# Attention and a GRU on one core: another order for the last batch, two more batches turned early, roots of norms ahead of GpSimd's normalisation

## The chip, the core and the metric

The kernel runs on one core of a Trainium2 chip. A core has TensorE (PE, matrix products; its weight loads are listed as PEld), VectorE (DVE), ScalarE (ACT), GpSimd (POOL) and SyncE (SP), each with an instruction queue that it works through in order. Products land in PSUM, eight banks of 2 KB per partition; all else lives in SBUF. The metric is the device time of one execution in microseconds.

## The reference

All arrays are float32. There are 16 batches of 256 positions of 512 features, and one row of conditions for each batch. The first half is attention with 16 heads of 32 features, the second a GRU over the 256 positions:

```python
scale, shift = split(cond @ W_emb + b_emb)
xn  = rms_norm(x, g_norm) * (1 + scale) + shift
q, k, v = heads(xn @ W_qkv)
q, k = rms_norm(q, g_q), rms_norm(k, g_k)          # per head
attn = softmax(q @ k.T * 32 ** -0.5)
o = attn @ v
x = x + o + o @ W_out
...
gi = x_t @ W_ih + b_ih ; gh = h @ W_hh + b_hh       # 256 steps
r = sigmoid(gi_r + gh_r) ; z = sigmoid(gi_z + gh_z)
n = tanh(gi_n + r * gh_n) ; h = (1 - z) * n + z * h
out_t = x_t + h
```

## The kernel before

**Attention, by batch and group.** A batch has two tiles of 128 positions. A group is four heads, so that a batch has four groups (g = 0 to 3) of 128 features. `logits` (L269) makes a group's four tiles of 128 x 512 logits, one in each of the PSUM banks lg0 to lg3. `maxima` (L292) takes the row maxima on VectorE, `exps` (L296) the exponentials and their sums on ScalarE: eight instructions of 256 columns. `normalize` (L306) takes the reciprocal of the sums on VectorE and has GpSimd multiply the eight halves by it, in place. In the next group's time `turn` (L316) transposes the normalised weights on TensorE, 64 rows at a time, into four banks; `put_turned` (L331) copies those to `attnT` in SBUF (one buffer), "v" on VectorE and "a" on ScalarE; `weigh` (L340) multiplies by v, and `put_weighed` (L356) copies the result into `oT`, which gathers [feature, position, batch] of all batches.

**The projections of the next batch ride along.** `slot0` to `slot3` (L375, L415, L436, L465) are the four groups of batch b, with the work of batch m = b + 1 written in between by hand: projections to q, k and v (`project`, L208: one step is four products of 128 x 32 by 512 columns, recorded as eight), the squares and sums of q and k, their roots and normalisation (`norm_qk`), and their turn into qT and kT (`turn_qk`, `put_qk`). Batch b + 2's x is turned (`turn_x`, `put_x`) in slot 0, and batch b + 3's is normalised in slots 1 to 3 (`norm_first`, `norm_apply`; the latter also loads the x of two batches later on SP's queue). For batch 0 and for batch 2's x there is nothing earlier: batch 0's slot 0 does all of batch 2's normalisation and turn.

**Roots.** `Rsqrt.first` (L138) makes the mean on VectorE (m) and, on ScalarE, exp(-0.5 ln) (L142, L143). `Rsqrt.second` (L145) refines it with three VectorE operations on small tiles (L147, L148, L150). In slots 1 and 2 `normalize` stands ahead of `second`.

**The banks.** Beside lg0 to lg3 there are four single banks A, X, Y, Z. q and k of the second tile, for instance, stand in Z and Y until `norm_qk` has read them, and the turn of q and k takes "ZY" next.

**The last batch** (b = 15) has no batch to project. `slot_last` (L492) turns the group before, takes maxima and exponentials, copies the turned weights (three on VectorE, one on ScalarE), normalises and weighs; in the last group half of the normalisation is VectorE's. Behind the loop the last group is turned and weighed.

**The GRU.** The output projection of 16 positions (`output_step`, wo, which has the identity added for the residual) and the input projection (`input_step`, wih) of a group of positions come as filler in the recurrence of the group before; for the first group they stand alone ahead of it: L670, first "o", then "gi". `put_block` (L680) transposes 8 positions of x into xT; `put_output` (L701) adds the output projection to it. The gates' products (L732) take three PSUM banks, "o" and "gi" two each, out of pools that are opened when attention's pools are closed.

**Order.** Inside `tc.manual_schedule` (L508, L779) TensorE, VectorE, ScalarE and GpSimd keep the order in which the program is written. SP, which issues most of the DMAs, is ordered by the scheduler. In the first part, weights and x are loaded in the order: four pieces of conditions (ScalarE's queue), w_emb (L75, both queues), x of batch 0, b_emb and g_norm (`rows`, L96, L97, SP's queue), then w_qkv (L103) by thirds, with x of batch 1 between the second and third. `rows` are transposed (L524) ahead of the embedding product (L528).

Of the kernel before, what the change touches and what calls it, by code (L numbers as in the profile page):

```python
# [19 lines left out]
def kernel(  # L20
# [51 lines left out]

    we = wpool.tile([P, KC, 2 * D], F32, tag="w_a", name="we")
    for k in range(KC):
        (nc.sync, nc.scalar)[k % 2].dma_start(we[:, k, :], w_emb[k * P : (k + 1) * P, :])  # L75

    work = ctx.enter_context(ExitStack())
    p1 = work.enter_context(tc.tile_pool(name="p1", bufs=1))
    p2 = work.enter_context(tc.tile_pool(name="p2", bufs=2))
    small = work.enter_context(tc.tile_pool(name="small", bufs=4))  # L80
    ps_lg = work.enter_context(tc.tile_pool(name="ps_lg", bufs=1, space=PSUM))
    ps = work.enter_context(tc.tile_pool(name="ps", bufs=1, space=PSUM))

# [8 lines left out]

    rows = p1.tile([12, P], F32, tag="qkn", name="rows", bufs=4)
    nc.sync.dma_start(rows[0:8, :], b_emb.rearrange("(m c) -> m c", c=P))  # L96
    nc.sync.dma_start(rows[8:12, :], g_norm.rearrange("(m c) -> m c", c=P))  # L97
    rows_b = p1.tile([26, P], F32, tag="qkn", name="rows_b", bufs=4)
# [170 lines left out]
    def logits(b, g):  # L269

        w = Group()
        w.b, w.g = b, g
        w.lg = [
            ps_lg.tile([P, NT, T], F32, tag=f"lg{i}", name=f"lg_{b}_{g}_{i}") for i in range(HG)
        ]
        for n in range(NT):
            for i in range(HG):
                r = slice(i * DH, (i + 1) * DH)
                nc.tensor.matmul(  # L279
                    w.lg[i][:, n, :],  # L280
                    qT[r, g, n * P : (n + 1) * P],
                    kT[r, g, :],
                    start=True,
                    stop=True,
                )
        w.neg = small.tile([P, HG, NT], F32, tag="neg", name=f"neg_{b}_{g}")
        w.den = small.tile([P, HG, NT], F32, tag="den", name=f"den_{b}_{g}")
        w.rden = small.tile([P, HG, NT], F32, tag="rden", name=f"rden_{b}_{g}")
        w.attn = [None] * HG
        return w  # L290
# [15 lines left out]
    def normalize(w, heads=range(HG), engine=nc.gpsimd):  # L306
        r = slice(heads[0], heads[-1] + 1)
        nc.vector.reciprocal(w.rden[:, r, :], w.den[:, r, :])  # L308
        for i in heads:
            for n in range(NT):  # L310
# [3 lines left out]
                )  # L314

    def turn(w, banks=("lg0", "lg1", "lg2", "lg3")):  # L316


        if w is None:
            return  # L320
        w.tp = [tile_ps(f"tpa_{w.b}_{w.g}_{i}", banks[i], (P, R, NT, NT, QR)) for i in range(HG)]
        for i in range(HG):
            for n in range(NT):
                for k in range(NT):
                    turn_block(
                        [w.tp[i // R * R + r][:, i % R, k, n, :] for r in range(R)],
                        w.attn[i][:, n, k * P : (k + 1) * P],
                    )
        w.attnT = p1.tile([P, HG, NT, T], F32, tag="attnT", name=f"attnT_{w.b}_{w.g}")

    def put_turned(w, engines):  # L331

        if w is None:
            return
        for i, e in enumerate(engines):
            h, r = i // R * R, i % R
            dst = w.attnT[:, h : h + R].rearrange("p h k (n r c) -> p h k n r c", n=NT, r=R)[:, :, :, :, r]
            (nc.scalar.copy if e == "a" else nc.vector.tensor_copy)(dst, w.tp[i])  # L338

# [15 lines left out]

    def put_weighed(w):  # L356
        if w is None:
            return
        nc.scalar.copy(oT[:, w.g, :, w.b], w.o)  # L359

# [14 lines left out]
    def slot0(b, w, prev, st):  # L375
        m = b + 1
        if b == 0:
# [3 lines left out]
            exps(w, range(HG))  # L381
            put_x(m, 0, st.tpx)
            put_v(b, 1, st.v1)
            st.q = project(m, 0, 0, range(KC), "A")
            norm_first(2)
            batches[2].rs.first()
            normalize(w)
            norm_apply(2, batches[2].rs.second())
            st.k = project(m, 0, 1, (0, 1), "X")
            tpx = turn_x(2, "YZ")  # L390
            put_x(2, 1, tpx)
            st.s0 = Stats(m, 0)
            st.s0.add(0, st.s0.square(0, st.q))
            put_x(2, 0, tpx)
            return
# [19 lines left out]
    def slot1(b, w, prev, st):  # L415
# [12 lines left out]
        st.s0.rs.first()  # L428
        normalize(w)
        st.s1 = Stats(m, 1)  # L430
        st.sq = st.s1.square(0, st.q1)
        weigh(prev, "Y")
        put_weighed(prev)
        st.rstd = st.s0.rs.second()

    def slot2(b, w, prev, st):  # L436
# [15 lines left out]
        if b + 3 < B:  # L452
            batches[b + 3].rs.first()
        normalize(w)
        weigh(prev, "X")
# [6 lines left out]
        st.accs = (st.q1, k)  # L462
        st.rstd = st.s1.rs.second()

    def slot3(b, w, prev, st):  # L465
# [25 lines left out]

    def slot_last(g, w, prev):  # L492

        turn(prev, "AXYZ")
        maxima(w, range(HG))
        exps(w, range(HG))
        put_turned(prev, "vvva")
        if g < NG - 1:
            normalize(w)
        else:  # L500
            normalize(w, (0, 1))
            normalize(w, (2, 3), nc.vector)
        weigh(prev, "A")
        put_weighed(prev)

    E = mybir.EngineType
    ORDERED = {E.PE, E.DVE, E.Activation, E.Pool}
    with tc.manual_schedule(engines=ORDERED):  # L508
# [12 lines left out]
        nc.vector.tensor_copy(h0T, tp)  # L521
        cols = const.tile([P, 38], F32, name="cols")
        tp = tile_ps("tp_rows", "Y")
        nc.tensor.transpose(tp[:, :12], rows, ident[:12, :12])  # L524
        nc.vector.tensor_copy(cols[:, :12], tp[:, :12])
        for k in range(KC):
            for j in range(4):
# [5 lines left out]
                    stop=(k == KC - 1),  # L533
                )
        norm_first(0)
        batches[0].rs.first()
        norm_apply(0, batches[0].rs.second())
        emb = p1.tile([P, 8, 32], F32, tag="sq", name="emb")
        nc.vector.transpose(emb.rearrange("p m b -> p (m b)"), pe)
# [16 lines left out]
        for c in range(KC):  # L556
            put_x(0, 0, tpx, (c,))
            put_x(0, 1, tpx, (c,), nc.scalar)
        q = project(0, 0, 0, range(KC), "Y")
        k = project(0, 0, 1, range(KC), "Z")  # L560
        tp = tile_ps("tp_rows_b", "lg3")
        nc.tensor.transpose(tp[:, :26], rows_b, ident[:26, :26])
# [6 lines left out]
        s0 = Stats(0, 0)  # L569
        s0.add(0, s0.square(0, q))  # L570
        s0.add(1, s0.square(1, k))
        s0.rs.first()
        norm_first(1)
        qk = norm_qk(0, 0, (q, k), s0.rs.second())
        batches[1].rs.first()
        q = project(0, 1, 0, range(KC), "A")
        s1 = Stats(0, 1)
        s1.add(0, s1.square(0, q))
        norm_apply(1, batches[1].rs.second())
        k = project(0, 1, 1, range(KC), "X")  # L580
        tq = turn_qk(0, 0, qk, ("lg0", "lg1"))
        tpx = turn_x(1, ("Z", "lg3"))
        v = project(0, 0, 2, range(KC), "Y")
        s1.add(1, s1.square(1, k))
        s1.rs.first()
        put_qk(0, 0, tq, nc.vector)
        put_qk(0, 1, tq, nc.scalar)
        put_x(1, 1, tpx, engine=nc.scalar)
        qk = norm_qk(0, 1, (q, k), s1.rs.second())
# [3 lines left out]
        put_qk(1, 1, tq, nc.scalar)  # L593
        put_v(0, 0, v)
        st.tpx = tpx

        prev = None
        for b in range(B):
            for g in range(NG):
                w = logits(b, g)  # L600
                if b + 1 < B:
                    (slot0, slot1, slot2, slot3)[g](b, w, prev, st)
                else:
                    slot_last(g, w, prev)
                prev = w
        turn(prev)
        put_turned(prev, "vava")
        weigh(prev, "X")
        put_weighed(prev)

# [29 lines left out]
    gru = ctx.enter_context(tc.tile_pool(name="gru", bufs=2))  # L640
    ps_g = ctx.enter_context(tc.tile_pool(name="ps_g", bufs=1, space=PSUM))
    ps_i = ctx.enter_context(tc.tile_pool(name="ps_i", bufs=2, space=PSUM))
    ps_o = ctx.enter_context(tc.tile_pool(name="ps_o", bufs=2, space=PSUM))

# [8 lines left out]
    gates = []  # L653
    for name in ("r", "z", "n"):
        gt = ps_g.tile([P, P], F32, tag=f"g{name}", name=f"g{name}")
        nc.vector.memset(gt, 0.0)
        gates.append(gt)

    TI = 16
    NI = T // TI  # L660
# [30 lines left out]
    def output_step(grp, i):  # L691

        m, k = divmod(i, KC)
        if k == 0:
            acc["o"] = ps_o.tile([P, TI * B], F32, tag="o", name=f"o_{grp}_{m}")
        product(
# [8 lines left out]
    def input_step(grp, i):  # L705
# [4 lines left out]
        if k == 0:  # L710
            acc["i"] = ps_i.tile([P, TI * B], F32, tag="gi", name=f"gi_{grp}_{m}")
        product(acc["i"], wih, m, k, xTs[grp][:, k].rearrange("p t b -> p (t b)"))
# [45 lines left out]
    def store_last(y, tl, n):  # L758

        tp = ps_o.tile([P, KC, P], F32, tag="o", name=f"tpy_{tl}")  # L760
        for q in range(KC):
# [17 lines left out]
    with tc.manual_schedule(engines=ORDERED):  # L779
        for i in range(TI // TG):  # L780
            put_block(i)
        for i in range(KC * KC):
            output_step(0, i)
            if i % KC == KC - 1:
                put_output(0, i // KC)
        for i in range(TI // TG, 2 * TI // TG):
# [97 lines left out]
```

## Time and profile before

| What | us |
| --- | --- |
| median of 3 runs (lowest, highest) | 1790.54 (1789.55, 1792.69) |
| the profiled execution, whole | 1791.88 |
| its span | 1790.1 |
| first logits of batch 0 start at | 36.52 |
| batch 0, slots 0 and 1 last | 11.18 and 11.70 |
| logits of batch 15 start at | 593.93 |
| first output projection starts at | 633.33 |
| first input projection starts at | 640.25 |
| recurrence starts at | 661.19 |

Busy over the span: TensorE 1731.6 us (97%), VectorE 1144.7 (64%), ScalarE 817.2 (46%), GpSimd 315.2 (18%). Shares of the whole span say little here, since the span has parts with different limits: a first part of loads and batch 0's projections, fifteen batches with projections in between, a last one without, and the recurrence, which takes 63% of the time. So the profile is read by stage. A chain of waits gives, in order of time, what each step waited for last; its columns are start, length, engine, tile, line and number of instructions. A table of stages gives each engine's busy time, the clock that TensorE was granted (1.00 is full) and the DMA engines' share. TensorE's products are pipelined, so a busy TensorE may still be stretched by a lower clock.

### The profile page before, as it was taken

To read this page: it belongs to the slowest core of one execution; us is meant where nothing else is said; L and a number is where in the kernel's file an instruction comes from. 1 tells how busy PE (TensorE), PEld (TensorE's weight loads), DVE (VectorE), ACT (ScalarE), POOL (GpSimd) and SP (SyncE) were. 2 spreads that over 40 slices of the span, in tenths; PEclk is the share of its full clock that TensorE was granted. 3 is DMA by queue.
4 is the path that set the end of the run, shared out by engine and by line. 5 is a ranking of instruction groups with operands and counts; after the bars stand their busy time and mean duration, and the time that the engine had idled before them with its cause. 6 is when DMAs were issued, how large, how long until landed. Compare 5 with 4: busy or idle time off the path is not lost.

```text
span 1790.1 us, 91923 instructions
## 1 busy us (share of the span) xinstructions
PE 1731.6 (97%) x40755; PEld 1190.4 (66%) x40755; DVE 1144.7 (64%) x3703; ACT 817.2 (46%) x2760; POOL 315.2 (18%) x769
## 2 busy tenths in 40 slices
PE   7999999999999799999999999999999999999975
PEld 2444444444444468888888888888888888888864
DVE  4777777777777635656656656566566666566555
ACT  4677777777777623333333332333333333333322
POOL 0343444433344400000000000000000000000000
PEclk9999999999999899999999999999999999999999
DMA  7200000000000110110011011001100100000000
GB/s 266 54 14 14 14 26 14 14 14 14 13 2 2 72 26 10 22 22 16 16 23 20 16 20 23 16 16 22 22 16 17 23 13 10 15 10 10 10 15 14
DMA packets 146222, 43.73 MB, mean 24 GB/s; under 512 B 137899, under 2 KB 138031, under 8 KB 145823
## 3 DMA queue, kind: packets, MB, share of 16 engines
q1 hardware_dynamic: 145375, 36.74, 8.8%
q8 instruction: 320, 5.24, 1.2%
q10 hardware_dynamic: 448, 1.10, 0.2%
q14 instruction: 79, 0.65, 0.1%
HBM read 29.41 MB, written 8.39 MB: 21 GB/s over the span
## 4 chain that ended last, share of the span: by engine, by line
PE 88%; DVE 8%; ACT 2%; issue 1%; DMA 0%; DVEq 0%; ACTq 0%; SPq 0%
PE gi L670 18%; PE qkv L214 15%; PE gr L732 13%; PE gn L732 13%; PE gz L732 12%; PE o L670 6%; PE tpa L188 3%; PE lg L279 3%; PE o L348 3%; DVE neg L294 2%; PE tpqk L188 1%; ACT attn L300 1%; DVE attnT L338 1%; DVE qkn L240 1%; DVE tr L744 1%
## 5 line engine op out<-in xcount | busy, mean ns | idle before, releaser
L670 PE MATMUL gi<-xT,wih 128*32 128x256 f32 x6144 | 364.6, 379 | 0.0
L214 PE MATMUL qkv<-wq,xnT 128*32 128x512 f32 x3072 | 355.9, 597 | 0.9 <-DVE xnT L206 0.7
L311 POOL TENSOR_SCALAR attn<-attn,rden 128x256 f32<-128x256 f32 x508 | 232.6, 480 | 394.6 <-DVE rden L308 267.7
L732 PE MATMUL gr<-whh,h 128*16 128x128 f32 x8160 | 272.2, 274 | 23.7 <-DVE h L836 23.5
L732 PEld LDWEIGHTS gr<-whh,h 128*16 128x16 f32 x8160 | 200.5, 96 | 105.8 <-DVE h L836 105.8
L838 POOL TENSOR_TENSOR y<-xT,h 128x64 f32<-128x64 f32 x255 | 81.9, 321 | 1069.2 <-DVE h L836 1031.9
L300 ACT ACTIVATE attn<-lg,neg 128x256 f32<-128x256 f32 x512 | 234.8, 485 | 77.1 <-DVE neg L294 61.3
L732 PE MATMUL gn<-whh,h 128*16 128x128 f32 x8160 | 269.5, 273 | 0.0
L732 PE MATMUL gz<-whh,h 128*16 128x128 f32 x8160 | 269.5, 273 | 0.0
L670 PEld LDWEIGHTS gi<-xT,wih 128*32 128x32 f32 x6144 | 195.9, 110 | 100.9
L807 ACT ACTIVATE r<-r 128x64 f32<-128x64 f32 x256 | 65.8, 257 | 377.7 <-DVE r L806 377.7
L744 DVE STREAM_TRANSPOSE tr<-gr 128x128 f32<-128x128 f32 x256 | 81.1, 317 | 237.6 <-PE gr L732 237.6
L732 PEld LDWEIGHTS gn<-whh,h 128*16 128x16 f32 x8160 | 224.7, 97 | 0.0
L732 PEld LDWEIGHTS gz<-whh,h 128*16 128x16 f32 x8160 | 224.7, 97 | 0.0
L214 PEld LDWEIGHTS qkv<-wq,xnT 128*32 128x32 f32 x3072 | 87.3, 109 | 181.8 <-issue 156.4
L294 DVE TENSOR_REDUCE neg<-lg 128x2 f32<-128x512 f32 x256 | 158.6, 680 | 52.4 <-PE lg L279 52.4
L714 ACT ACTIVATE gi<-gi,cols 128x256 f32<-128x256 f32 x192 | 91.2, 475 | 166.8 <-PE gi L670 166.8
L744 DVE STREAM_TRANSPOSE tr<-gn 128x128 f32<-128x128 f32 x256 | 81.1, 317 | 76.0 <-PE gn L732 76.0
L670 PE MATMUL o<-oT,wo 128*32 128x256 f32 x2048 | 121.7, 379 | 0.7 <-ACT oT L359 0.7
L338 DVE COPY attnT<-tpa 128x512 f32<-128x512 f32 x132 | 84.7, 684 | 54.0 <-ACT sq L225 37.2
L300 ACT ACTIVATION_READ_ACCUMULATOR attn<-lg,neg 128x1 f32 x512 | 110.8, 216 | 0.0
L813 ACT ACTIVATE n<-n 128x64 f32<-128x64 f32 x256 | 65.6, 256 | 98.8 <-DVE n L812 96.1
(102 smaller groups left out, 1743.4 us busy)
## 6 DMA issues: line engine op xcount, KB each, us to landing
x<-in_x_dram SPq DMA_DIRECT2D x16, 512.0 KB, 3.7
xin<-in_x_dram SPq DMA_DIRECT2D x256, 32.0 KB, 1.9
out_dram<-osb SPq DMA_DIRECT2D x248, 32.0 KB, 1.9
wq<-in_L_cond_W_qkv_dram SPq DMA_DIRECT2D x12, 256.0 KB, 4.2
wih<-in_L_cond_W_ih_dram SPq DMA_DIRECT2D x4, 768.0 KB, 10.6
whh<-in_L_cond_W_hh_dram SPq DMA_DIRECT2D x4, 768.0 KB
we<-in_L_cond_W_emb_dram SPq DMA_DIRECT2D x2, 512.0 KB, 5.1
we<-in_L_cond_W_emb_dram ACTq DMA_DIRECT2D x2, 512.0 KB, 6.3
```

The lines of the kernel that those rows point to most:

```text
L188: nc.tensor.transpose(dst[r], src[q], ident[q, q])
L214: nc.tensor.matmul(a[32 * j : 32 * j + 32, :], batches[b].xnT[:, k, n * P + 32 * j : n * P + 32 * j + 32], wq[:, k, s * D : (s + 1) * D], ...
L294: nc.vector.tensor_reduce(w.neg[:, i, :], w.lg[i], AX.X, ALU.max, negate=True)
L300: nc.scalar.activation(a[:, n, :], w.lg[i][:, n, :], AF.Exp, bias=w.neg[:, i, n : n + 1], accum_out=w.den[:, i, n : n + 1],)
L311: engine.tensor_scalar(w.attn[i][:, n, :], w.attn[i][:, n, :], w.rden[:, i, n : n + 1], 1.0, ALU.mult, ALU.mult,)
L338: (nc.scalar.copy if e == "a" else nc.vector.tensor_copy)(dst, w.tp[i])
L670: nc.tensor.matmul(acc[32 * j : 32 * j + 32, :], w[:, k, m * P + 32 * j : m * P + 32 * j + 32], rhs, start=(k == 0), stop=(k == KC - 1),)
L714: nc.scalar.activation(gis[grp][:, m].rearrange("p t b -> p (t b)"), acc["i"], AF.Identity, bias=bcols[:, m : m + 1],)
L732: nc.tensor.matmul(gates[g][32 * j : 32 * j + B, :], hT[:, k, :], whh[:, k, g * D : (g + 1) * D].rearrange("p (q j c) -> p j q c", q=KC, c ...
L744: nc.vector.transpose(tr.rearrange("p q b -> p (q b)"), gates[g])
L807: nc.scalar.activation(r, r, AF.Sigmoid)
L838: (nc.gpsimd if t + 1 < T else nc.vector).tensor_tensor(y[:, :, tl * B : (tl + 1) * B], xTs[grp][:, :, ti, :], h, ALU.add)
```

## The change

In the first part:

- `rows` are loaded on ScalarE's queue, ahead of w_emb, and transposed behind the embedding product; their copy to SBUF comes behind batch 0's normalisation.
- Batch 1's norm and its application are moved ahead of batch 0's projections, its turn (banks lg0, lg1) behind q and k; batch 2's norm, application and turn (banks Y, Z) are done here too. v goes to bank lg2, and the copies of batch 1's x are split between ScalarE and VectorE.
- Slot 0 of batch 0 only copies batch 2's turned x (both banks on VectorE), and normalises behind the sum of the square.

In slots 1 and 2, `normalize(w)` stands behind `rs.second()`:

```diff
         st.s0.rs.first()
-        normalize(w)
         st.s1 = Stats(m, 1)
         st.sq = st.s1.square(0, st.q1)
         weigh(prev, "Y")
         put_weighed(prev)
         st.rstd = st.s0.rs.second()
+        normalize(w)
```

The last batch has a function of its own. The turn is split into two pairs of heads with two banks each, weighing goes one more group back, and the output projection of the first 16 positions is made by its four blocks of features, in lg0 and lg1, as those blocks become ready; the GRU part then adds two tiles of 512 columns to xT:

```diff
+    def project_first(k):
+        if k == 0:
+            first.extend(tile_ps(f"first_{i}", f"lg{i}", (P, 2, TI * B)) for i in range(KC // 2))
...
+    def last_batch(prev):
+        b, before = B - 1, None
+        w = logits(b, 0)
+        for g in range(NG):
+            if before:
+                weigh(before, "Z")
+            turn_pair(prev, 0, "AX")
+            maxima(w, (0, 1))
+            exps(w, (0, 1))
+            if before:
+                put_weighed(before, nc.vector)
+            turn_pair(prev, 1, "YZ")
+            maxima(w, (2, 3))
+            exps(w, (2, 3))
+            put_turned_bank(prev, 0, nc.vector)
             normalize(w, (0, 1))
-            normalize(w, (2, 3), nc.vector)
-        weigh(prev, "A")
+            put_turned_bank(prev, 2, nc.vector)
+            put_turned_bank(prev, 1, nc.scalar)
+            put_turned_bank(prev, 3, nc.scalar)
+            if g < NG - 1:
+                normalize(w, (2, 3))
+                before, prev, w = prev, w, logits(b, g + 1)
+        project_first(0)
+        project_first(1)
+        normalize(w, (2,), nc.vector)
+        normalize(w, (3,))
+        turn_pair(w, 0, ("lg2", "lg3"))
+        turn_pair(w, 1, "AX")
+        weigh(prev, "Z")
+        put_turned(w, "vava")
         put_weighed(prev)
+        weigh(w, "Y")
+        put_weighed(w, nc.vector)
+        project_first(2)
+        project_first(3)
```

The PSUM pools of attention stay open, and the GRU part takes its banks from them: the gates A, X and Y, "o" lg0 and lg1, "gi" Z and lg2.

```diff
-        for i in range(KC * KC):
-            output_step(0, i)
-            if i % KC == KC - 1:
-                put_output(0, i // KC)
+        for i, o in enumerate(first):
+            a = xTs[0][:, 2 * i : 2 * i + 2].rearrange("p q t b -> p q (t b)")
+            nc.vector.tensor_tensor(a, o, a, ALU.add)
```

## The prediction

> **What bounds the kernel now.** I read the table of stages first, to see where TensorE is short of work; then the chain that ended last, stage by stage; then the engines' own orders in time, for slack. Times are us of the profiled execution: 1791.88 in all, of which the span is 1790.1. The median of the three runs is 1790.54, 1.34 less; I sum against 1791.88 and take the 1.34 off at the end.
>
> The first lines are stages (start:end and length, busy time of each engine with its instructions, granted clock, DMA): a steady batch, the last batch with the first output projection, one group of the last batch, the first input projection.
>
> ```profile
> 299.00:336.00 37.00, 36.84 (x504) 17.29 (x500) 28.30 (x63) 28.41 (x96) 14.70 (x33) 1.00 0.05 16
> 593.93:640.25 46.32, 34.05 (x436) 19.24 (x436) 24.36 (x49) 22.02 (x77) 15.19 (x33) 0.78 0.23 78
> 602.00:610.90 8.90, 6.34 (x70) 3.71 (x68) 4.48 (x8) 4.83 (x18) 3.52 (x9) 0.69 0.03 12
> 640.40:661.00 20.60, 20.60 (x392) 12.37 (x384) 1.64 (x3) 5.21 (x11) 0.00 (x0) 1.00 0.22 35
> ```
>
> A steady batch (36.8) is TensorE's; so is the recurrence from 661 on, which the change leaves as it is. The last batch is not: one group takes 8.9 and no engine is busy for more than 6.34 of it, on a granted clock of 0.69. Its chain:
>
> ```profile
> 602.09 2.06 PE lg L279 x16
> 604.15 0.68 DVE neg L294
> ...
> 604.92 0.55 ACT attn L300 x2
> ...
> 607.09 1.59 ACT attn L300 x7
> 608.68 0.48 ACT attnT L338
> ...
> 609.20 1.73 PE o L348 x12
> 610.93 2.06 PE lg L279 x16
> ```
>
> Logits, maxima, exponentials, the copy of the turned weights queued behind the exponentials on ScalarE, weighing, the next logits: one thing after another, every group. The first batch has a chain of its own, of which this is the middle:
>
> ```profile
> 42.62 1.24 ACT xs L165 x4
> ...
> 45.76 1.32 DVE xs L172 x2
> ...
> 47.12 0.67 PE tpx L188 x14
> ```
>
> TensorE waits for batch 2's normalisation there. The only wait left in a steady batch is the end of this chain, in slot 2 and slot 3:
>
> ```profile
> 326.40 0.44 DVE u_qk L147
> ...
> 327.73 2.39 DVE neg L294 x4
> 330.12 1.21 DVE qkn L240 x2
> 331.33 0.04 issue
> 331.37 0.71 PE tpqk L188 x15
> ```
>
> The turn of q and k starts at 330.94, stops after one block and goes on at 331.37, when the qkn copies have given back its bank.
>
> **The change, part by part.**
>
> *Roots ahead of the normalisation (slots 1 and 2).* Each group's three root operations (L147, L148, L150) take 0.36, 0.42 and 0.42 while GpSimd normalises (317.54 to 321.19, 326.31 to 329.96), and 0.19 each in the first part, where GpSimd rests. From 326.40 they last 1.33 until the maxima start at 327.73. Ahead of GpSimd I take the spacing of the first part, 0.22 each: 0.66. The reciprocal, 0.20 and now hidden in the wait for ScalarE's roots, comes behind them: 1.33 - 0.66 - 0.20 = 0.47 earlier. TensorE can win no more than its stall: 16 blocks take 0.93 (330.94 to 331.87) against 0.55 for the 16 of x (304.38 to 304.93), so 0.35 to 0.4. I take 0.35 in each of 15 batches: **5.3**; ends 0 and 0.47 x 15 = 7. In slot 1 the projection of v reaches its bank at 322.25, after it came free (about 321.9), so nothing is won there. The price: GpSimd starts about 1.05 later in slot 2 (327.35, ends at 331.0) and 0.85 later in slot 1 (ends at 322.05). The turns that read its result start at about 331.5 and 323.1, so the delay is covered by 0.5 and 1.1.
>
> [...]
>
> *Two batches turned in the first part.* Today slot 0 of batch 0 lasts 36.52 to 47.70 = 11.18 and slot 1 lasts 47.70 to 59.40 = 11.70. Without batch 2's work in slot 0, TensorE has logits 1.08 and nine projection steps of 0.89 (40 records in 4.45): 9.1, gain **2.1**. VectorE's two copies of x (2.6) and the square's sum still stand ahead of the reciprocal; with them GpSimd runs from about 8.9 to 12.6 after slot 0's logits, and the turn that needs it comes at 14.6. So slot 1 takes what steady slot 1 takes (308.86 to 317.59 = 8.73): gain **2.95**. Ends for the pair: 4 and 5.3.
>
> In the first part I walk TensorE. The rows of b_emb and g_norm no longer hold it: the wait for g_norm ends at 10.03 today, and the embedding product runs 10.35 to 13.96. The product can start when h0T is there (8.1) and needs its last weights, issued on ScalarE's queue at 3.5, 6.3 to landing; the two rows' issues now stand before them (0.35 + 0.25). So it ends at about 12, then VectorE's four steps as today (14.03 to 15.17) from 12.2, and q starts at 13.9 instead of 15.74: 1.85 won. Added: turning x of batches 1 and 2, of which only batch 1's was there: 0.6, and a stall for batch 2's xs, because VectorE has both batches' copies (4 x 0.33), sums and roots to do: about 0.6. That leaves **0.6**, logits at 35.9. Batch 1's normalisation now waits for x_1 behind wq's second third on SP's queue. SP loses two issues and its early wait (4.98), so x_1 lands between 15.6 and 18.2 by the bytes moved (3.7 MB by 12.0, 5.05 MB by 18.0); at 18.2 it costs 0.6 more. A slower SP is thus 0; a quicker one 1. SP's loads of x_3 and x_4 come earlier and compete with nothing due.
>
> *The last batch.* Weighing goes one group back, banks split in pairs, and logits follow only the exponentials. Eight exponentials take 3.75. When they end, five of eight logits products are left: 5/8 of 1.08 at full clock, of 2.06 at the low one: 0.7 to 1.3; then maxima 0.7 and 0.1 of hand-overs. A round is 5.25 to 5.85. ScalarE's two copies (1.07) fit into that gap. Where weighing (0.98 at full clock, some 2.4 for 16 records at the low one: 12 took 1.73 to 1.92) is late, VectorE's copy of it holds up the second pair of maxima by up to 0.9: worst 6.8. I take 5.7.
>
> The first exponentials start 1.96 after the first logits (593.93 to 595.89), the fourth group's at 1.96 + 3 x 5.7 = 19.1. From there: turns done at 2.2; two projection parts of 1.73 (128 records took 7.11) plus 0.7 for a clock still low, 6.4; two turns 1.15, 7.5; weighing 0.98, 8.5; two copies of turned weights on each engine, 1.3, for which attnT must be read out first, 9.8; weighing 1.0, 10.8; two projection parts, 14.3; hand-over to the sum over xT, 0.2: 14.5. The input projection starts at 33.6 instead of 46.3: gain **12.7**. Ends: 15.2 (5.25, no low clock) and 8 (6.8, and 1 more at the end). The memsets, transposes and x blocks on VectorE (2.1) lie beside the last two projection parts. The first output projection was 7.11 alone and now half lies in the tail; the two sums over 512 columns (0.7 each) overlap it, but for the second, which the first two input steps (1.7) cover.
>
> The row says that the clock falls to 0.69 with no idle stretch over 2.6. [...]
>
> *The banks of the recurrence* are seven as before, two each for o and gi, three gates: 0.
>
> **Sum.** 0.6 + 2.1 + 2.95 + 5.3 + 12.7 = 23.7: 1791.88 - 23.7 = 1768.2; on the median's scale 1766.8, so **1767**.
>
> **Rivals** (on the same scale).
> 1. The last batch becomes TensorE's on a low clock, rounds of 6.8: gain there 8, **1771.5**. For it: 0.69 today. Against: denser work.
> 2. The roots win nothing in the steady batch (GpSimd or a bank ends last in place of the qkn copies): **1772**. For it: the 0.5 of slack.
> 3. The last batch keeps its rounds of 8.9, some copy still queued ahead of the logits: **1779.5**. Against: nothing but the exponentials holds the banks of logits.
> 4. Slower: the reciprocal sits behind the roots in VectorE's queue, and the roots behind ScalarE. Today's GpSimd could start 1.55 (slot 2) and 1.95 (slot 1) later before a turn waits, 1.75 in the mean; at 2.6 later it passes the turns' starts by 0.85, 30 times: 25, which eats everything else. If it slipped behind the next group's four maxima (2.39), that is 3.4 later, 1.65 x 30 = 50 lost against 18.4 won elsewhere: **1822**. Against: the order has the reciprocal ahead of the maxima, and ScalarE's roots take 0.6.
>
> Chances: forecast 0.55, rivals 0.2, 0.12, 0.08, 0.04; 0.01 for rivals 2 and 3 together with a first part that wins nothing, about 1790. The range joins the bounds: gains of 1.0 + 5.3 + 7 + 15.2 = 28.5 and of 0 + 4 + 0 + 8 = 12, that is 1762 to 1778.5; I keep **1761 to 1778**, which leaves out rivals 3 and 4. A measurement can tell 0.2%, 3.6 us, from no change: faster 0.95, same 0.01, slower 0.04.
>
> **What would show it.** Batch 15's logits every 5.3 to 6 us, granted clock above 0.69; the input projection 33 to 35 after its first logits; root operations of 0.19; the 16 blocks of tpqk without a gap; slots 0 and 1 of batch 0 near 9.1 and 8.7; q of batch 0 near 13.9. Wrong if turns wait for GpSimd in slot 2 or 3, or ScalarE waits for the second pair of maxima in the last batch.

## The result, and the profile after

The changed kernel takes **1775.9 us** (median of 4 runs, 1775.18 to 1776.63) against 1790.36 for the kernel before (4 runs, 1789.55 to 1792.69): a ratio of 0.9917, interval 0.9900 to 0.9934, so 14.5 us are won. The forecast was 1767 in a range of 1761 to 1778. The profiled execution took 1775.52, its span is 1773.7; against the profiled execution of before, 1791.88, that is 16.4. The medians are 14.5 apart, since the profiled execution of before lies 1.5 above its median and that of the changed kernel 0.4 below. The stages below add up to the 16.4.

First the same four stages that the prediction shows of before, in the changed kernel's table of stages: a steady batch, the last batch with the first output projection, one group of the last batch, the first input projection (start:end and length, busy time of PE, PEld, DVE, ACT and POOL with their instructions, granted clock, DMA share, GB/s).

```profile
295.26:331.88 36.62, 36.62 (x500) 17.17 (x496) 27.18 (x62) 28.40 (x96) 14.68 (x33) 1.00 0.05 17
588.16:623.26 35.10, 32.35 (x436) 19.57 (x433) 22.57 (x49) 21.78 (x77) 16.09 (x35) 0.85 0.24 93
595.46:601.27 5.81, 5.62 (x72) 3.73 (x68) 4.43 (x10) 4.83 (x18) 3.07 (x7) 0.71 0.18 73
623.26:644.22 20.96, 20.96 (x394) 12.62 (x396) 1.90 (x3) 5.21 (x11) 0.00 (x0) 1.00 0.32 51
```

A steady batch is now TensorE's without a gap, 36.62 of 36.62. The last batch went from 46.32 to 35.10, and its group from 8.90 to 5.81, of which TensorE is busy for 5.62: it has become TensorE's, on a clock of 0.71. The chain of waits through it (start, length, engine, tile, line, instructions):

```profile
593.93 1.13 PE lg L279 x10
595.05 1.42 PE o L358 x16
596.47 1.94 PE tpa L188 x32
...
598.57 1.12 ACT attn L301 x5
599.69 0.04 issue
599.74 0.77 PE lg L279 x8
...
605.16 1.54 PE lg L279 x10
606.70 1.86 PE o L358 x16
608.57 1.90 PE tpa L188 x31
610.47 4.63 PE first L506 x64
...
617.39 0.70 DVE attnT L341
...
619.89 3.45 PE first L506 x62
623.34 20.85 PE gi L713 x384
```

Weighing (o) takes 1.42 at a granted clock of 0.66 and 1.86 at 0.50, and 1.04 at 616.26 at 1.00; the first half of the output projection takes 4.63 at 0.77, the second 3.45 at 1.00. The same work took longer where the granted clock was lower. The chain of the first part:

```profile
0.74 3.94 DMA we<-in_L_cond_W_emb_dram
4.68 0.02 issue
4.70 6.31 DMA x<-in_x_dram
...
16.12 8.31 PE qkv L214 x64
24.43 0.69 PE tpx L188 x16
...
39.23 1.15 PE lg L279 x16
```

Of before it had the row of g_norm and then the embedding product in this place. Now x of batch 0 is late: its load starts at 4.70, behind the landing of a part of w_emb, where it started at 1.67 before. The first logits come at 39.23, later than before (36.52), and not earlier.

| stage | before | after | won | forecast |
| --- | --- | --- | --- | --- |
| start to first logits of batch 0 | 36.52 | 39.23 | -2.71 | 0.6 |
| slot 0 of batch 0 | 11.18 | 8.94 | 2.24 | 2.1 |
| slot 1 of batch 0 | 11.70 | 8.68 | 3.02 | 2.95 |
| slot 2 of batch 0 to logits of batch 15 | 534.53 | 531.31 | 3.22 | 5.3 |
| logits of batch 15 to first input projection | 46.32 | 35.10 | 11.22 | 12.7 |
| first input projection | 20.94 | 20.96 | 0 | 0 |
| recurrence | 1128.9 | 1129.5 | -0.6 | 0 |

The sum is 16.4 against 23.7. Two steps carry the difference: the first part, 3.3 worse, and the roots, 2.1 worse; the last batch lacks 1.5. The 0.6 in the recurrence are not explained; the kernels below, which all have the changed recurrence, take 1129.4 to 1130.5 for it, so all of them are a little longer than before.

### The profile page after: what moved, and what is told of

Read it like the earlier page. It is cut to its first block, busy times and chain, and to the rows that moved or that the text cites. A ratio compares the mean times of both kernels' runs of the same rounds, so it can differ in the third digit from the quotient of the medians.

```text
span 1773.7 us, 91931 instructions
## 1 busy us (share of the span) xinstructions
PE 1729.7 (98%) x40755; PEld 1189.8 (67%) x40755; DVE 1126.3 (64%) x3703; ACT 816.9 (46%) x2760; POOL 316.8 (18%) x771
## 4 chain that ended last, share of the span: by engine, by line
PE 94%; DVE 3%; ACT 1%; issue 1%; DMA 1%; DVEq 0%; ACTq 0%
PE qkv L214 19%; PE gi L713 18%; PE gr L775 13%; PE gn L775 13%; PE gz L775 11%; PE o L713 6%; PE tpa L188 4%; PE lg L279 4%; PE o L358 4%; PE tpqk L188 1%; DVE tr L787 1%; ACT attn L301 1%; PE tpx L188 1%; PE first L506 0%; DMA x<-in_x_dram 0%
## 5 line engine op out<-in xcount | busy, mean ns | idle before, releaser
L713 PE MATMUL o<-oT,wo 128*32 128x256 f32 x1920 | 114.6, 379 | 0.0
```

What stands on the lines that cost most here:

```text
L713: nc.tensor.matmul(acc[32 * j : 32 * j + 32, :], w[:, k, m * P + 32 * j : m * P + 32 * j + 32], rhs, start=(k == 0), stop=(k == KC - 1),)
```

## Experiments

My theory after the result: (a) the two `rows` loads, now ahead of w_emb, hold up x of batch 0, and with it everything; (b) the roots win 3, because the stall was smaller than I read; (c) the last batch loses to the granted clock. Rivals: for (a) the added turns and copies of batch 2; for (b) that GpSimd's later start takes something back; for (c) that a copy or the order of the tail holds it up at any clock. All medians stand against the kernel before on the same chip: 1789.78 for runs 1 to 4, 1790.43 for 5 to 8, 1790.58 for 9 to 11. In brackets behind a median are its number of executions, its ratio to the kernel before and the interval of the ratio. These intervals overlap for most kernels that lie 3 apart, so I call two kernels different where no execution of the one lies among those of the other, and say so where one does. Times within a kernel's profile are those of one execution. The mean granted clock of every execution is on record as well.

### 1. `rows` behind x of batch 0

```diff
-    rows = p1.tile([12, P], F32, tag="qkn", name="rows", bufs=4)
-    nc.scalar.dma_start(rows[0:8, :], b_emb.rearrange("(m c) -> m c", c=P))
-    nc.scalar.dma_start(rows[8:12, :], g_norm.rearrange("(m c) -> m c", c=P))
...
     load_x(0)
 
+    rows = p1.tile([12, P], F32, tag="qkn", name="rows", bufs=4)
+    nc.scalar.dma_start(rows[0:8, :], b_emb.rearrange("(m c) -> m c", c=P))
+    nc.scalar.dma_start(rows[8:12, :], g_norm.rearrange("(m c) -> m c", c=P))
```

> The changed kernel, with only the two loads of rows moved behind the load of batch 0's x in program order (still on ScalarE's queue). Theory: the first part lost 2.7 us because loads share eight completion semaphores, so that a load waits until the one eight ahead of it has landed; the two rows pushed x_0 behind the eighth place, and it was issued at 4.70 instead of 1.67. Then x_0 is issued by 2.2 here, lands by about 8.5 instead of 11.0, q of batch 0 starts at 13.5 to 14.5, the first logits at 36 to 37.5 instead of 39.2, and the time is 1773 to 1774. Rival: the bytes ahead of w_qkv's second third and x_1 set the start in any case; then the first logits stay within 0.7 of 39.2 and the time at 1775 to 1776.

1775.29 (4 runs; ratio 0.9917, 0.9903 to 0.9930): no gain that can be told from the changed kernel. But the mechanism shows. x of batch 0 is issued at 1.66 and q starts at 14.25 instead of 16.12. First logits: 38.69. What is late next is x of batch 1, in the chain and in TensorE's order (start, length, engine, line, operation; idle time before it and its releaser in brackets):

```profile
14.48 5.87 DMA x<-in_x_dram
```

```profile
23.49 1.05 PE L188 MATMUL tpx<-ident,xs 64*128 64x64 f32 x16 [2.14 <-DVE xs L172]
```

It is issued at 14.48 behind the second third of w_qkv and lands at 20.35; q and k are done at 21.34, and TensorE waits 2.14 for its norm. So (a) is half right: one late load hid another.

### 2. and 3. Roots undone, first part undone

```diff
+        normalize(w)
         st.s1 = Stats(m, 1)
...
         st.rstd = st.s0.rs.second()
-        normalize(w)
```

> The changed kernel with normalize again ahead of the roots in slots 1 and 2. By the traces of the two kernels the roots are worth 0.2 us a batch (36.84 against 36.62): 3.2 us over fifteen batches, so 1779.1, and the stall of the turn of q and k is back (0.93 instead of 0.74 for 16 blocks). The prediction had 5.3: 1781.2. Rival: the roots win nothing and the 3.2 come from elsewhere: 1775.9 and a batch of 36.6.

1779.28 (5 runs; 0.9938, 0.9924 to 0.9951), 3.4 slower than the changed kernel. In its profile 551.77 lie between the first logits of batch 0 and those of batch 15, against 548.93: **2.84** for the roots. Part of the rest is the last batch, 36.47 against 35.10, which this edit does not touch.

The second kernel has the loads, batch 0's projections and slot 0 of the kernel before, with roots and last batch of the changed one. The core of the edit:

```diff
     load_x(0)
+    rows = p1.tile([12, P], F32, tag="qkn", name="rows", bufs=4)
+    nc.sync.dma_start(rows[0:8, :], b_emb.rearrange("(m c) -> m c", c=P))
...
-            for r in range(R):
-                put_x(2, r, st.tpx)
+            norm_first(2)
+            batches[2].rs.first()
+            normalize(w)
+            norm_apply(2, batches[2].rs.second())
+            st.k = project(m, 0, 1, (0, 1), "X")
+            tpx = turn_x(2, "YZ")
...
-        norm_first(1)
-        batches[1].rs.first()
-        norm_apply(1, batches[1].rs.second())
         q = project(0, 0, 0, range(KC), "Y")
         k = project(0, 0, 1, range(KC), "Z")
-        tpx = turn_x(1, ("lg0", "lg1"))
```

> The changed kernel with the first part and batch 0's slot 0 of the kernel before; roots and last batch stay changed. Theory: the first logits come 2.7 earlier (36.5), slots 0 and 1 take 5.3 longer (22.6 to 22.9 together): 2.5 us slower than the changed kernel, 1778.4. By the prediction's terms (0.6 + 2.1 + 2.95) it would be 5.65 slower, 1781.5. Rival: part of the loss is in the recurrence or in run to run differences; then the time is within 1 of 1775.9.

1779.12 (5 runs; 0.9932, 0.9919 to 0.9944), 3.2 slower, though one of the five took 1774.50, at a mean clock of 0.997 against 0.995 in the others. Its first logits come at 36.18 and slots 0 and 1 take 11.18 and 11.89: slot 1 ends at 59.25, in the changed kernel at 56.85. So the changed first part is worth 2.4 as it stands, where the forecast had 5.65. The last batch took 36.46 here.

### 4. The last batch alone

Both edits of 2 and 3 together.

> The kernel before with the last batch's new order alone (first part and roots undone). If the parts add up, it is 3.2 + 2.5 slower than the changed kernel: 1781.6, that is 8.8 to 11 faster than before, and the stretch from batch 15's first logits to the first input projection is 35.1 as in the changed kernel. The prediction had 12.7 for this part alone: 1777.7. [...]

1780.84 (5 runs; 0.9945, 0.9933 to 0.9958), 8.9 faster than before. From the logits of batch 15 to the first input projection it took 37.88, on a granted clock of 0.50 from 600 to 605. Four kernels with the changed kernel's last batch, instruction by instruction, thus took 34.89 (run 1), 36.47, 36.46 and 37.88 for it: the order of the work does not settle that time. Executions of one kernel lie as far apart: the five of this run go from 1777.12, at a mean clock of 0.998, to 1782.45, at 0.995. Its slot 1 of batch 0 is that of the kernel before, but took 10.31 at full clock where before took 11.70, the last 2.92 of them at half clock.

### 5. x of batch 1 early as well

```diff
         if i == 0:
+            load_x(1)
             for r, g in ((0, g_q), (1, g_k)):
...
-        if i == 1:
-            load_x(1)
```

> As rows_behind_x, and the load of batch 1's x moved up from behind w_qkv's second third to behind its first. Theory: with x_0 on time, batch 1's x is the next late thing (landed at 20.4 there, and TensorE stood 2.1 ahead of its turn and 1 more behind it); issued four loads of w_qkv and four small ones earlier, it lands by 16 to 17, the turn of batch 1 follows q and k without a wait, unless k waits for w_qkv's second third, and the first logits come at 36 to 37 instead of 38.7: 1773 to 1774. Rival: w_qkv's second third is late in its place (half a megabyte later, 1.3): first logits at 37.5 to 38.5, 1775.

1773.36 (4 runs; 0.9905, 0.9892 to 0.9919), 2.5 less than the changed kernel. The chain of the first part:

```profile
14.05 7.09 PE qkv L213 x64
21.14 0.69 PE tpx L187 x16
...
35.95 1.10 PE lg L278 x13
```

q at 14.05, q and k in 7.09 without a stall, turns at 21.14, logits at 35.95: the prediction's walk (13.9 and 35.9), once both loads are early. Slot 1 ends at 53.56, 5.7 earlier than with the first part of before. The rival of (a), the added turns and copies, cost 1.1, about the 1.2 that the prediction gave them: 14.8 from the end of q and k to the logits, 13.7 before. But its last batch took 36.49 on a low clock, which ate 1.4 of the gain.

### 6. VectorE's copy of the weighed group behind the second maxima

In the changed kernel the second pair of exponentials of the last round waited 1.24 for maxima, which stood behind VectorE's copy of a weighing on the low clock.

```diff
-            if before:
-                put_weighed(before, nc.vector)
-            turn_pair(prev, 1, "YZ")
             maxima(w, (2, 3))
+            if before:
+                put_weighed(before, nc.vector)
+            turn_pair(prev, 1, "YZ")
```

> The changed kernel with VectorE's copy of the weighed group (last batch) behind the second pair of maxima instead of ahead of it, and with it TensorE's second pair of turns. Theory: ScalarE's waits in the middle of the exponentials (0.36, 0 and 1.24 in rounds 2 to 4) go, so the stretch from batch 15's first logits to the first input projection shortens from 35.1 by up to 1.6. Rival: the clock sets it; the copy waits for a slow weighing, and what is won there is lost as the turn's second pair and the next logits come later on TensorE: no change within the 34.9 to 37.9 seen over four kernels. Either way within 2 us of 1775.9.

1775.15 (5 runs; 0.9916, 0.9902 to 0.9930): no difference that can be told. Yet in its profiled execution (1773.92) the clock stayed at 1.00, all rounds took 5.34 or 5.35, and the stretch 32.68. The other four executions have mean clocks of 0.995 to 0.998. So the profiled execution shows what a full clock gives, and the others that this place of the copy does not bring it about.

### 7. Another order of the tail

```diff
         project_first(0)
-        project_first(1)
         normalize(w, (2,), nc.vector)
         normalize(w, (3,))
+        weigh(prev, "Z")
+        put_weighed(prev)
+        project_first(1)
         turn_pair(w, 0, ("lg2", "lg3"))
         turn_pair(w, 1, "AX")
-        weigh(prev, "Z")
         put_turned(w, "vava")
-        put_weighed(prev)
+        project_first(2)
         weigh(w, "Y")
         put_weighed(w, nc.vector)
-        project_first(2)
```

> The changed kernel with another order behind the last logits: weighing of group 2 between the first two projection parts, so that attnT is read out before the last turns are copied, and the third projection part between the last turns and the last weighing. Theory: the 0.97 in which TensorE stands idle ahead of the last weighing (attnT's single buffer) goes, and the copies hide behind the projection part: from the fourth group's first exponentials to the first input projection 15.4 to 15.7 instead of 16.6, 1775.0. Rival: the weighing waits for ScalarE's last two copies (they end 1.1 behind its last exponentials) where it is now placed, and the second and third projection parts run on the low clock: no gain.

1777.19 (5 runs; 0.9929, 0.9917 to 0.9942), not better. In its profile the first logits come as late as 40.62, which this edit does not touch. The tail from the last group's exponentials took 14.67, as long as at full clock with the old order (14.69 in run 6). TensorE's idle time only moved: 0.95 ahead of the last weighing (0.97 in the changed kernel), and 0.71 and 0.50 ahead of what follows it.

### 8. More work for TensorE

If the clock is low because TensorE waits between the logits, work that nobody needs should make the kernel faster. The second pair of turns is repeated in the first three rounds; it writes the same values to the same banks.

```diff
-            turn_pair(prev, 1, "YZ")
+            turn_pair(prev, 1, "YZ", (4, 3, 3, 1)[g])
```

> The changed kernel with idle work added on TensorE in the last batch: the second pair of turns is made 4, 3 and 3 times instead of once in rounds 1 to 3 (same blocks into the same banks, 0.58 each at full clock; 4.1 in all). Theory: the clock falls because TensorE waits for exponentials; with the waits filled, the granted clock stays 1.00, logits, weighing and turns run at full speed, and the rounds go from 5.8, 5.8 and 5.4 to 5.3 in spite of the added work: the stretch to the first input projection shrinks from 35.1 to 33 to 34, 1774 to 1775. Rival: what bounds the rounds is ScalarE and the hand-overs, or the clock falls anyway: the added work comes on top, the stretch is 36 to 39, 1777 to 1780.

**1772.68** (4 runs; 0.9904, 0.9890 to 0.9918), 3.2 less than the changed kernel, with its first part unmended (first logits at 38.90). Windows of 5 us in x1_early, then in this kernel, both from 5.1 after the first logits of batch 15:

```profile
590.00:595.00 5.00, 5.00 (x36) 2.35 (x37) 1.77 (x4) 3.54 (x14) 3.03 (x7) 0.50 0.66 270
595.00:600.00 5.00, 4.78 (x64) 3.21 (x60) 4.13 (x9) 3.45 (x13) 2.82 (x7) 0.82 0.00 0
```

```profile
593.00:598.00 5.00, 4.76 (x91) 3.27 (x91) 3.60 (x7) 4.38 (x18) 3.00 (x7) 1.00 0.65 267
598.00:603.00 5.00, 4.75 (x88) 3.19 (x86) 4.10 (x10) 4.38 (x19) 3.67 (x8) 1.00 0.01 3
```

The rounds of x1_early, without the repeats, took 5.87, 6.69 and 5.68. With the repeats the clock is 1.00 in every window to 620, the rounds take 5.34, 5.42 and 5.42, the tail 13.77, and the stretch 31.90. This is no matter of the one profiled execution: the mean clock is 0.998 to 1.000 in all 17 executions of the four kernels with the repeats (runs 8 to 11), and 0.994 to 0.998 in 36 of the 37 executions of the eight kernels that have the new last batch without them.

How the clock falls can be read off its changes. In every profile here they lie a whole number of 3.41 us apart; in the changed kernel at 595.49, 598.91, 605.73 and 612.56. Stages of that length, from the changed kernel:

```profile
588.66:592.08 3.42, 2.84 (x47) 1.82 (x42) 2.75 (x5) 2.63 (x11) 1.76 (x4) 1.00 0.92 370
592.08:595.49 3.41, 2.95 (x26) 1.60 (x30) 1.98 (x6) 2.79 (x11) 2.90 (x7) 1.00 1.02 425
595.49:598.90 3.41, 3.41 (x49) 2.47 (x41) 2.85 (x7) 3.05 (x13) 0.77 (x2) 0.50 0.29 117
598.90:602.32 3.42, 3.23 (x48) 1.87 (x45) 2.44 (x6) 2.80 (x11) 3.32 (x8) 1.00 0.00 0
602.32:605.73 3.41, 2.87 (x38) 1.82 (x34) 2.76 (x7) 3.41 (x14) 1.66 (x4) 1.00 0.02 5
605.73:609.14 3.41, 3.41 (x34) 1.49 (x31) 1.80 (x4) 2.27 (x9) 2.36 (x6) 0.50 0.00 0
```

and from run 6, cut where the clock would have changed (found from its fall at the end of the run):

```profile
589.62:593.03 3.41, 2.81 (x47) 1.80 (x40) 2.89 (x5) 2.63 (x11) 1.61 (x4) 1.00 0.95 384
593.03:596.44 3.41, 2.98 (x26) 1.57 (x30) 1.99 (x6) 2.79 (x11) 3.04 (x7) 1.00 1.00 416
596.44:599.86 3.42, 2.47 (x46) 1.52 (x38) 3.27 (x7) 3.42 (x16) 1.34 (x4) 1.00 0.26 104
```

So in these profiles the granted clock kept its value, 1.00 or 0.50, for 3.41 us or a multiple of it. In the kernels with the changed last batch each fall within it follows a stage in which TensorE was busy for 2.5 to 3.0 of the 3.41, with no recorded idle piece over 0.5; the stage at half clock is then filled, or nearly, by the slowed work, and one to three such stages pass before it is full again (10.24 us in run 4). So it may matter where the round's thin stretch lies against this grid; that this makes the same last batch differ by 3 is not shown. It can't be all: 592.08 to 595.49 of the changed kernel and 593.03 to 596.44 of run 6 are nearly alike in every column, and the one is followed by half clock, the other not. Run 6 has stages of 2.47 without a fall, and run 10, which has the repeats, one of 2.06 with 1.35 idle in one piece. So the repeats keep the clock, but that they do it by filling the idle places is not shown. What sets the granted clock stays open.

### 9. to 11. The parts together

Runs 5 and 8 together:

> Both mended parts together: x of batch 1 loaded early and the two rows behind x of batch 0 (x1_early), and the second pair of turns of the last batch repeated 4, 3 and 3 times (clock_kept). If the first part and the last batch's clock are separate causes: first logits at 36.0 as in x1_early, the last batch's stretch (first logits to first input projection) 31.9 as in clock_kept, granted clock 1.00 in its windows, and a median of 1775.9 - 3.3 - 3.2 = 1769.4. Rival: the repeats helped in clock_kept only by the phase in which the last batch happened to fall; then the stretch is 35 to 36.5 again with windows below 0.8, and the median 1773 to 1774.

**1769.6** (4 runs; 0.9888, 0.9875 to 0.9902), against 1769.4 worked out: the two causes are separate and add up. First logits 35.73, stretch 31.89 (584.71 to 616.60), and the clock at 1.00:

```profile
588.00:593.00 5.00, 4.71 (x74) 2.88 (x72) 3.42 (x8) 4.38 (x19) 3.65 (x8) 1.00 0.99 404
593.00:598.00 5.00, 4.78 (x90) 3.22 (x88) 4.18 (x9) 4.37 (x18) 2.85 (x7) 1.00 0.06 22
```

It is the fastest kernel of this study, 6.3 below the changed one. All its executions lie below those of run 8; one of run 5, at the highest mean clock of that kernel (0.998), lies among them. With run 6's place of the copy too:

> As best, with VectorE's copy of the weighed group behind the second maxima too (weighed_behind). If the clock is kept by the repeats, VectorE's copy no longer waits on slow products, and its place is worth nothing: 1769.4, rounds of 5.35. If the copy still holds up the second maxima at full clock, the rounds get 0.05 shorter and the median 1769.2; if TensorE's wait for the copy ahead of the second turn pair (0.95 in weighed_behind) now counts, because the repeated turns stand behind it, rounds are 5.5 or more and the median 1770.

1772.77 (4 runs; 0.9902, 0.9889 to 0.9916), 3.2 slower than run 9 by the medians; its fastest execution, 1771.45, lies just below run 9's slowest, 1771.69. The clock is 1.00 here too; the wait counts:

```profile
594.78 1.72 PE L187 MATMUL tpa<-ident,attn 64*128 64x64 f32 x47 [0.95 <-DVE oT L368]
```

Behind the wait now stand the repeats, and behind them the next logits, which start at 596.43 and at 602.29, so that a round takes 5.86 and the stretch 33.70. The other 1.4 is first part (0.55) and scatter.

Run 9 with the conditions in one load in place of four:

```diff
-    for k in range(KC):
-        nc.scalar.dma_start(cond_sb[k * B : (k + 1) * B, :], cond[:, k * P : (k + 1) * P])
+    nc.scalar.dma_start(cond_sb, cond.rearrange("b (k p) -> k b p", p=P))
```

> As best, with the conditions in one load in place of four, which frees three places among the loads ahead. If each load waits for the one eight ahead of it to land, w_emb's later pieces and x_1 are issued earlier; the embedding product ends earlier by up to 1 and the first logits come at 35 to 36: 1768.4 to 1769.4. Rival: one load of 64 rows scattered by position lands later than the four small ones, and h0T, so the embedding product, later: first logits at 37, 1770.4.

1773.33 (5 runs; 0.9909, 0.9896 to 0.9923), slower than run 9 but for one execution. The first logits come at 36.63, near the rival's 37, but by another road than the rival's: all parts of w_emb and x of batch 0 are under way together, and x takes 7.93 to land, at 9.60. The profiled execution (1770.85) is the lowest of the five; what the others lost is not in its trace.

## Why the prediction was right, and where it was wrong

The sign, the size within the range, and the order of the terms held. The time lies near the slow end of the range, and of the five terms only the two for slots 0 and 1 came as worked out: 16.4 were won where the sum had 23.7. By its own steps:

**First part: wrong.** The step that failed is "The rows of b_emb and g_norm no longer hold it ... q starts at 13.9", together with "SP loses two issues and its early wait (4.98)". I counted what two more issues cost ScalarE's queue (0.6) and left x of batch 0 where it was. SP's early wait did not go away: it passed to the load that now stood in its place in the count. In the records of both traces the first 28 loads signal through eight semaphores in turn (numbers 100 and 102 to 108); the first eight loads wait for none, and each of the other 20 waits for the semaphore of the load eight ahead. Lines of SP's order, from before and then from the changed kernel (start, length, queue, line, load):

```profile
1.67 0.43 SPq L88 DMA_DIRECT2D x<-in_x_dram  x1
4.98 0.35 SPq L96 DMA_DIRECT2D rows<-in_L_cond_b_emb_dram  x1
```

```profile
4.70 0.39 SPq L93 DMA_DIRECT2D x<-in_x_dram  x1
```

Two loads put ahead moved x of batch 0 from the eighth place (semaphore 108, no wait) to the tenth (102, whose first load is the part of w_emb that lands at 4.68), and from 1.67 to 4.70. The embedding product did end at about 12 (12.43), as worked out, and was no longer what was late. x of batch 1 landed by 19.84, after the 15.6 to 18.2 given. Run 5 wins back 3.28 of the missing 3.31 by the places of loads alone.

Of the 3.31, 2.2 are q's late start (16.12 against 13.9). The other 1.22 are a longer q and k (8.31 against 7.09), and these are TensorE's pace, not a wait. Stages from the changed kernel, then from run 7, whose first part is the same program (columns as above):

```profile
16.12:18.64 2.52, 2.52 (x12) 0.65 (x16) 0.90 (x3) 1.03 (x3) 0.00 (x0) 1.00 0.98 328
18.64:21.16 2.52, 2.52 (x28) 0.78 (x24) 0.00 (x0) 1.32 (x4) 0.00 (x0) 1.00 1.03 375
```

```profile
16.75:20.80 4.05, 4.05 (x20) 1.09 (x24) 0.91 (x3) 1.12 (x4) 0.00 (x0) 0.50 0.94 299
20.80:24.85 4.05, 4.05 (x44) 1.24 (x40) 1.54 (x6) 2.23 (x7) 0.00 (x0) 1.00 1.03 378
```

The changed kernel's trace has no clock on record before 18.64, where the table prints 1.00; its first record says full clock from 18.64 on. Until there a group of four products starts every 0.86, as in run 7 at a recorded 0.50, and from there every 0.43. Half of the 2.52 is 1.26, which accounts for the 1.22. The five kernels whose loads are placed as in the changed one run at full clock only from 18.64 to 20.80 on, after q's start, and their q and k take 8.31 to 9.57; the other kernels, the one before among them, reach it before q starts, and their q and k take 7.09. In the five, TensorE stands for 1.1 to 1.8 in the middle of the embedding product, waiting for the last part of w_emb. Whether that pause is what delays the clock was not tested.

**Slots 0 and 1 of batch 0: right in size.** 2.24 and 3.02 against 2.1 and 2.95. Of the 3.02 in slot 1, some 1.4 are a cause that the prediction does not name: in the kernel before the granted clock is 0.50 from 56.49 to 59.90. Run 4 has the same slot 1 at full clock, 10.31 instead of 11.70. The prediction's number holds since it compared with a steady slot at full clock.

**Roots: mechanism right, size wrong.** The mis-sized term is "0.35 in each of 15 batches". VectorE's order in a steady batch:

```profile
321.92 0.19 DVE L147 SCALAR_TENSOR_TENSOR u_qk<-y_qk 128x32 f32<-128x32 f32 x1 [0.36 <-ACT y_qk L143]
322.15 0.19 DVE L148 TENSOR_TENSOR u_qk<-u_qk,m_qk 128x32 f32<-128x32 f32 x1
322.37 0.19 DVE L150 SCALAR_TENSOR_TENSOR y_qk<-u_qk,y_qk 128x32 f32<-128x32 f32 x1
322.48 0.19 DVE L309 RECIPROCAL rden<-den 128x8 f32<-128x8 f32 x1
```

The operations take 0.19, spaced by 0.22, as worked out, where in the kernel before they took up to 0.43 while GpSimd normalised (326.40 to 327.73). And the stall is gone (TensorE's order):

```profile
326.46 0.96 PE L188 MATMUL tpqk<-ident,qkn 64*128 64x64 f32 x16
327.20 1.23 PE L188 MATMUL tpa<-ident,attn 64*128 64x64 f32 x32
```

But 16 turns of q and k without a stall take 0.74, from 326.46 to the next operation, and not the 0.55 of x that I compared them with. The row to compare with was in the trace of before: the second turn of q and k, 333.09 to 333.85. So the stall was 0.93 - 0.74 = 0.19, times 15 = 2.9; run 2, in whose trace the stall is back, measured 2.84. GpSimd ends at 326.51 and the turn that reads its result starts at 327.20: the cover held, and rival 4 did not come.

GpSimd's later end shows in slot 3, in two batches: the first root operation of x (L147) takes 0.29 at 70.30 and 0.23 at 509.64, both times until GpSimd's normalisation ends (70.59 and 509.87). In steady batches it takes 0.15 (at 326.57, with GpSimd done at 326.51). Nothing waits for it: the 16 turns of q and k beside it take the usual 0.74.

**Last batch: right in kind, 1.5 short.** The rounds took 5.34, 5.81 and 5.42, against 5.7 taken. What was mis-sized is the tail, 16.6 against 14.5: the step "two projection parts of 1.73 ... plus 0.7 for a clock still low" gave 6.4 to a point that is reached at 8.4 (615.10), since weighing and turns were at half clock too, and the exponentials of the second pair came 1.24 late behind VectorE's copy. At full clock the tail is 13.8 to 14.7 (runs 8 and 6). By the prediction's own terms the bounds come to 8.5 and 14.8, and not to 8 and 15.2. They were sound: 8.4 is the worst of the kernels with this last batch (run 4), and run 8 reaches 46.32 - 31.90 = 14.4 with more work.

That the new last batch could keep the full clock, as in the bound of 15.2, was my estimate. The profiles of runs 6 and 8 show it at 1.00; in those of the changed kernel and of run 4 it fell to 0.50: no stage ahead of a fall was idle, the thinnest was busy for 2.52 of 3.41 (run 4), the others for 2.87 and 2.95.

**Rivals.** Rival 1 (the last batch TensorE's on a low clock) came in its mechanism, at 5.8 in one round in place of 6.8; in the profiles of five other kernels with this last batch a round took 6.7, and in run 4 two took 7.2. Rival 2 is half true: 2.9 of 5.3. Rival 3 did not come.

## What to carry to other kernels

- A load that is moved ahead of others moves all of them back in the order of loads. Here two loads moved x of batch 0 from the eighth place to the tenth, and its issue from 1.67 to 4.70. Count the loads up to the first one that somebody waits for; the step after it may be late as well (x of batch 1 behind x of batch 0), so mend and look again.
- The size of a stall is the difference to the same operation on the same tiles without one, and not to a like operation on others.
- Read the granted clock in short stages, and ahead of its first record the pace of like products. Here a last batch that left TensorE short of work ran in part at 0.50 (595.49 to 598.90 and 605.73 to 612.56 in the changed kernel), and 4.1 us of useless turns were worth 3.2.

## What the runs showed of the hardware

- The granted clock changed between 1.00 and 0.50, each change a whole number of 3.41 us after the one before. In the new last batch half clock came after stages that were busy for 2.5 to 3.0 of 3.41, without an idle piece over 0.5, though not after each of them. Where the repeats filled the rounds' stages to 3.1 or more, it did not come in three profiles of three; in run 10 it did not come either, with stages down to 2.06.
- The same last batch took 34.89 to 37.88 in six kernels that differ only ahead of it, one profiled execution each. Executions of one kernel differ as much (run 4: 1777.12 to 1782.45), so this can't be put down to the edits.
- The changed kernel's first part ended at 38.90 to 40.62 in five kernels that have it, and at 35.73 to 36.28 in three with x of batch 1 early. The five differ in two things: q starts at 14.51 to 16.75, as loads land, and q and k take 8.31 to 9.57, as the full clock comes at 18.64 to 20.80.
